# A two-layer graph kernel in fp32: row sums of layer 0 on ScalarE, block transposes moved into the projection, sums of v in the room of the blocks

## The chip, the cores and the metric

The kernel runs on one core of one Trainium2 chip. A core has five engines with queues of their own, each worked off in order: TensorE (PE, matrix products; its weight loads are shown as PEld), VectorE (DVE), ScalarE (ACT), GpSimd (POOL) and SyncE (SP, which here only issues DMA transfers). The metric is the device time of one execution in microseconds (us), the median of several runs. Before the change it is 1717.73 us (three runs, 1717.66 to 1717.78).

## The reference

Inputs are x (64 graphs x 256 nodes x 512 features), a 0/1 adjacency matrix adj (256 x 256), three 512 x 512 weights Wq, Wk, Wv for layer 0, and a weight and a bias for layer 1. All is fp32.

```python
# layer 0
h = relu(layernorm(x))
q, k, v = h @ Wq.T, h @ Wk.T, h @ Wv.T
rel = adj.T * (q @ k.T)                      # 256 x 256 for each graph
rel = rel / norm(rel, axis=2)                # by rows
x = x + rel @ v
# layer 1
h = relu(layernorm(x))
x = x + (adj @ h) @ weight + bias
```

## The kernel before

The 64 graphs are worked off as 32 pairs. A tile of a pair has 128 partitions and, for x and h, four chunks of 512 elements (two graphs x two halves of the nodes). Wq and Wk are folded into one matrix M beforehand (`before_pairs`), so a pair needs G = M h, v, the scores h G, attention, and for layer 1 a gather (adj h) and a mix (times the weight).

Most products run as Winograd's 2 x 2 scheme: seven block products instead of eight (`winograd_steps`). They accumulate in three PSUM banks in the order bank_a, bank_c, bank_a, bank_c, bank_a, bank_b, bank_a; after each product the bank is emptied at once by `take`, by a ScalarE copy if it is the first value of its output block, else by a VectorE add. A later product into the same bank waits until that read is done. The operands of the scheme are sums and differences of blocks, four VectorE steps each: `right_operands` (L133 to L136) and `left_factors` (L158 to L161).

After a start (`first_pairs`) a steady step (`steady(i)`, 28 of them) works on several pairs at once, in this order on TensorE:

- `attend_and_v(i)`: attention of pair i and v of pair i+1, product by product in turn (L465 and L217, tiles of v and of x_ring)
- `scores(i+1)` (L229)
- `project_g(i+2)` (L205)
- `gather(i)` (L522, tiles py, yt)
- `mix(i)` (L217, tiles yt, ys, w)

`last_pairs` ends the run. The order on TensorE, VectorE and ScalarE is the program's own, written by hand: each stage takes a table `side`, and the work listed under slot n is issued right behind the stage's product n and its `take`. So a list such as `2: [end] + sums[1:2]` is a piece of an engine's queue, and an instruction that waits holds up all that stands behind it on its engine.

What else runs in a steady step: the norm of layer 0 for pair i+3 (`ln0`: bn_stats and bn_aggr on VectorE, L248 and L249, root on ScalarE, L253, relu on ScalarE, L260), the norm of layer 1 for pair i (`ln1`, the same lines, then an upper and a lower half of h: a ScalarE cast, L499, and a VectorE difference, L503) and the bias add on GpSimd (L495). h of pair i+3 is transposed in two moves: `place_blocks` sends its 32 x 32 blocks to transposed places in the tile `blocks` by 16 DMA transfers on SP's queue (L299), and `transpose_blocks` turns each on VectorE (L309, eight steps), giving `ht`; its four sums are called `sums`. The scores are masked (L375), their rows squared and summed on ScalarE (L380, into a tile `square` that nothing reads), scaled (L389), placed by 16 transfers (L396) and turned (L399).

Tiles come from pools. Tiles with one tag share one room (pool `work`): "hy" holds h of a pair and then yt; "ys" holds the sums of g (`g_operands`) and those of yt; "gt" holds the sums of v (`attend_operands`, tile vt). The adjacency matrix has a room of its own.

Of the kernel before, what the change touches and what calls it, by code (L numbers as in the profile page):

```python
# [19 lines left out]
def kernel(  # L20
# [36 lines left out]
    nc = tc.nc  # L57
    P = 128
    B, N, D = x.shape
    DC = D // P  # L60
    NC = N // P
# [29 lines left out]
    wq_sb = work.tile([P, DC, D], F32, tag="g", name="wq_sb")  # L91
    wk_sb = twice.tile([P, DC, D], F32, tag="v", name="wk_sb")
    wv_sb = work.tile([P, DC, D], F32, tag="h2", name="wv_sb")
    adj_sb = const.tile([P, NC, N], F32, name="adj_sb")
    w_sb = const.tile([P, DC, D], F32, name="w_sb")
    bias_bc = const.tile([P, D], F32, name="bias_bc")
    nc.scalar.dma_start(out=adj_sb, in_=adj.rearrange("(c p) n -> p c n", p=P))
# [20 lines left out]
    def flat(t):  # L118
        return t.rearrange("p b c d -> p (b c) d")
# [24 lines left out]
    def run(steps):  # L144
        for step in steps:
            step()
# [90 lines left out]
    def norm(src):  # L237
# [25 lines left out]

        return [(lambda c=c: chunk(c)) for c in range(TC)], root, end, relu


    def ln0(i):
# [7 lines left out]
        return chunks, root, end, [(lambda c=c: relu(h[:, c, :], c)) for c in range(TC)]  # L275

    def new_ht(i):
        return twice.tile([P, DC, NC, NB * P], F32, tag="ht", name=f"ht_{i}")
# [49 lines left out]
        winograd(product_tokens_moving(HL[i], m_right), take, side)  # L328
        G[i] = g

    def g_operands(i, tag="ys"):

        g, t = G[i], work.tile([P, 3, HC, HT_], F32, tag=tag, name=f"gt_{i}")
        G[i], steps = right_operands(
            lambda j, k: g[:, j * HC : (j + 1) * HC, k], [t[:, n] for n in range(3)]
        )
        return steps

    def v_products(i):
# [15 lines left out]
    def scores(i, side={}, by_matmul=False):  # L355


        left, right = HL.pop(i), G.pop(i)
        rel = work.tile([P, NB, NC, N], F32, tag="rel", name=f"rel_{i}")
        placed = work.tile([P, NB, NC, NC, P], F32, tag="placed", name=f"placed_{i}")  # L360
        turned = work.tile([P, NB, NC, NC, P], F32, tag="turned", name=f"turned_{i}")
        square = work.tile([P, N], F32, tag="square", name=f"square_{i}")
        rn = small.tile([P, NB, NC], F32, tag="rn", name="rn")
        R[i] = turned, rel

        def take(t, k, bank, first):
            dst = rel[:, :, k, ts(t, P)]
            src = bank[:, :HT_].rearrange("p (b m) -> p b m", b=NB)
            if first:
                nc.scalar.copy(dst, src)  # L370
            else:
                nc.vector.tensor_add(dst, src, dst)  # L372

        def mask(k):
            nc.vector.tensor_mul(  # L375
                rel[:, :, k], rel[:, :, k], adjt_sb[:, k : k + 1, :].to_broadcast([P, NB, N])
            )

        def square_sum(b, k):
            nc.scalar.activation(square, rel[:, b, k], AF.Square, accum_out=rn[:, b, k : k + 1])  # L380

        def root():
            nc.scalar.activation(rn, rn, AF.Sqrt)

        def inverse():
            nc.vector.reciprocal(rn, rn)

        def scale(b, k):
            nc.scalar.activation(rel[:, b, k], rel[:, b, k], AF.Copy, scale=rn[:, b, k : k + 1])  # L389

        def place():
            rv = rel.rearrange("p b k (t m) -> p (b k t) m", m=P)
            pv = placed.rearrange("p b k t n -> p (b k t) n")
            for j in range(P // S):
                for k in range(P // S):
                    nc.sync.dma_start(out=pv[ts(j, S), :, ts(k, S)], in_=rv[ts(k, S), :, ts(j, S)])  # L396

        def turn(b, k):
            nc.vector.transpose(turned[:, b, :, k], placed[:, b, k])  # L399

        def each(f):
            return [(lambda b=b, k=k: f(b, k)) for k in range(NC) for b in range(NB)]

        def turn_at_once():
            for b in range(NB):
                pt = ps_m.tile([P, T], F32, tag="pm", name="pr")
                for t in range(NC):
                    for k in range(NC):
                        nc.tensor.transpose(
                            pt[:, ts(t * NC + k, P)], rel[:, b, k, ts(t, P)], ident  # L410
                        )
                nc.scalar.copy(turned[:, b].rearrange("p t k n -> p (t k n)"), pt)

        winograd(product_of_tokens(left, right), take, side)
        if by_matmul:
            masks = [lambda: mask(0), lambda: mask(1)]
# [26 lines left out]
    def attend_operands(i):  # L443


        turned, rel = R.pop(i)
        v, t = V.pop(i), work.tile([P, 3, NB, HD], F32, tag="gt", name=f"vt_{i}")
        room = rel.rearrange("p b k m -> p (b k m)")
        left, left_steps = left_factors(
            lambda n, m: turned[:, :, m, n],  # L450
            [room[:, ts(j, HT_)].rearrange("p (b n) -> p b n", b=NB) for j in range(3)],
        )
        right, right_steps = right_operands(
            lambda m, k: v[:, :, m, ts(k, HD)], [t[:, n] for n in range(3)]
        )
        R[i] = left, right
        return right_steps, left_steps
# [98 lines left out]
    def layer_1(parts):  # L556

        root, end, relus, uppers, lowers = parts
        return {
            0: [root, end, relus[0], relus[1]],  # L560
            1: [uppers[0], uppers[1], lowers[0]],
            2: [relus[2], lowers[1]],
            3: [relus[3], uppers[2], uppers[3]],
            4: [lowers[2]],
            5: [lowers[3]],
        }

    def before_pairs():
# [42 lines left out]
        def take(t, k, bank, first):  # L611
# [12 lines left out]
            1: [left_steps[2], right_steps[2]],  # L624
            2: stats[0:2] + [lambda: load(1, nc.scalar)],
            3: [left_steps[3]] + stats[2:4] + [root, right_steps[0], lambda: load(2, nc.scalar)],
            4: [transpose_wv, end] + relus + [right_steps[3]],
            5: m_steps[0:3],
            6: m_steps[3:4],
        }, early=True)  # L630

# [26 lines left out]
    def first_pairs(exact):  # L658
# [46 lines left out]
        if exact:  # L705
# [2 lines left out]
            1: [inverse], 3: scales + [place], 4: turned3[0:1], 5: turned3[1:2], 6: turned3[2:4],  # L708
        }))
        v_steps, rel_steps = attend_operands(1)  # L710
        y_steps = gather(0, exact, {
            0: turned3[4:8], 1: v_steps[0:1], 2: v_steps[1:3], 3: v_steps[3:4],
        })
        run(y_steps[0:2])
        mix(0, {0: y_steps[2:3], 1: y_steps[3:4], 4: turns, 5: rel_steps})
        return sums3

    def steady(i, exact, sums):

        gs = g_operands(i + 1)
        stats0, root0, end0, relus0 = ln0(i + 3)
        stats, root, end, relus, uppers, lowers = ln1(i, exact)
        halves = [stats[b * NC + t] for t in range(NC) for b in range(NB)]
        attend_and_v(i, {
            0: stats0[0:2], 1: stats0[2:4] + [root0], 2: [end0, relus0[0]] + gs[0:2],
            3: relus0[1:2] + gs[2:3], 4: relus0[2:3] + gs[3:4], 5: relus0[3:4] + sums[0:1],
            6: halves[0:2],
        })  # L730
        place_blocks(i + 3)
        masks, squares, norm_root, inverse, scales, place, turns = scores(i + 1, {
            0: halves[2:3], 1: halves[3:4] + [root], 2: [end] + sums[1:2], 3: relus[0:1],
            4: relus[1:2], 5: uppers[0:1], 6: uppers[1:2] + sums[2:4],
        })
        v_steps, rel_steps = attend_operands(i + 1)
        project_g(i + 2, {
            0: masks[0:1] + lowers[0:1] + relus[2:3],
            1: masks[1:2] + lowers[1:2] + relus[3:4],
            2: uppers[2:4] + squares[0:2] + v_steps[0:1],  # L740
            3: lowers[2:3] + squares[2:4] + [norm_root],
            4: lowers[3:4] + [inverse] + scales + [place],
            5: v_steps[1:2],
            6: v_steps[2:4],
        })
# [82 lines left out]
```

## Time and profile before

| | |
|---|---|
| median of 3 runs | 1717.73 us |
| profiled execution | 1717.2 us |
| its span, first to last instruction | 1715.1 us |
| granted TensorE clock | 0.999 |
| busy share: PE, PEld | 99%, 89% |
| busy share: DVE, ACT, POOL | 79%, 39%, 12% |
| one steady step (attend stage starts at 857.58 us, the next at 909.9) | 52.3 us |
| its stages: attend and v, scores, project_g, gather, mix | 18.1, 6.3, 12.1, 3.7, 12.1 us |

All times inside the execution count from the start of the span. In a row of the profile, "out<-in" are tiles by their names in the program, "L252" is a line of the kernel, and in lists of waits the engine and tile left of the arrow waited for those on its right. An engine's busy share says little by itself here: what matters is which engine another one waits for at a given point.

### The profile page before, as it was taken

What the parts mean: (1) busy time and instruction counts of PE and PEld (TensorE: products, weight loads), DVE (VectorE), ACT (ScalarE), POOL (GpSimd) and SP (SyncE); (2) the same over time, 40 slices, a digit from 0 to 9 for tenths busy, and PEclk for the clock granted to TensorE, in tenths of its full rate; (3) what the DMA queues carried; (4) which work ended last, traced back from release to release, by engine and by line L of the source; (5) the groups of instructions that cost most, each with busy time, mean ns of one, the idle gap of its engine ahead of it and who ended that gap; (6) DMA issues with size and microseconds to landing.
All of it is one profiled execution on the core that took longest, in us unless ns stands there. A gap on an engine that the chain in (4) does not pass through costs nothing.

```text
span 1715.1 us, 24952 instructions
## 1 busy us (share of the span) xinstructions
PE 1702.2 (99%) x9170; PEld 1518.2 (89%) x9170; DVE 1360.1 (79%) x2672; ACT 663.3 (39%) x1387; POOL 201.2 (12%) x167
## 2 busy tenths in 40 slices
PE   9999999999999999999999999999999999999998
PEld 7979998989898999889898989998889989899986
DVE  6778888878888888888787888888888888887655
ACT  4434433444333344334443333443343433334331
POOL 0011100111101111001111011110011110011111
PEclk9999999999999999999999999999999999999999
DMA  7423333233332233332233322333322334222011
GB/s 239 65 33 80 77 86 76 51 59 80 81 86 66 45 74 77 86 77 56 53 81 80 87 67 48 71 76 85 78 59 49 81 80 87 68 53 41 28 24 63
DMA packets 425972, 122.34 MB, mean 71 GB/s; under 512 B 398064, under 2 KB 399344, under 8 KB 425840
## 3 DMA queue, kind: packets, MB, share of 16 engines
q1 hardware_dynamic: 413248, 80.28, 25.1%
q0 software_dynamic: 8432, 32.51, 5.0%
q10 hardware_dynamic: 4160, 7.87, 1.3%
q8 instruction: 74, 1.21, 0.3%
q14 instruction: 58, 0.48, 0.1%
HBM read 38.27 MB, written 33.55 MB: 42 GB/s over the span
## 4 chain that ended last, share of the span: by engine, by line
PE 96%; DVE 3%; ACT 0%; DMA 0%; issue 0%; ACTq 0%; DVEq 0%
PE bank_a L217 25%; PE bank_c L217 13%; PE bank_a L205 13%; PE py L522 7%; PE bank_a L229 7%; PE bank_b L217 7%; PE bank_c L205 6%; PE bank_a L465 6%; PE bank_c L229 3%; PE bank_b L205 3%; PE bank_c L465 3%; PE bank_b L229 2%; PE bank_b L465 1%; DVE st L248 1%; PE pu L430 0%; DMA wk_sb<-in_L_gnn_Wk_dram 0%
## 5 line engine op out<-in xcount | busy, mean ns | idle before, releaser
L346 ACT COPY v<-bank_a 128x512 f32<-128x512 f32 x96 | 56.2, 586 | 676.6 <-PE bank_a L217 676.6
L495 POOL TENSOR_TENSOR x_ring<-x_ring,bias_bc 128x512 f32<-128x512 f32 x128 | 176.3, 1396 | 822.6 <-DVE rel L372 548.8
L248 DVE BATCH_NORM_STATS2 st<-x_ring 128x6 f32<-128x512 f32 x256 | 171.5, 670 | 0.4
L539 DVE TENSOR_TENSOR x_ring<-bank_a,x_ring 128x512 f32<-128x512 f32 x128 | 88.2, 689 | 57.9 <-PE bank_a L217 57.9
L522 PE MATMUL py<-adjt_r,h 128*128 128x256 f32 x1024 | 130.4, 285 | 0.0
L522 PEld LDWEIGHTS py<-adjt_r,h 128*128 128x128 f32 x1024 | 123.9, 189 | 1.6
L217 PE MATMUL bank_a<-w_t,ys 128*128 128x256 f32 x512 | 121.3, 380 | 1.7 <-DVE x_ring L539 1.7
L217 PE MATMUL bank_a<-wv_t,hs 128*128 128x256 f32 x512 | 121.0, 379 | 0.0
L205 PE MATMUL bank_a<-hs,m_t 128*128 128x256 f32 x512 | 121.0, 379 | 0.0
L260 ACT ACTIVATE h2c<-x_ring,nb,rs 128x512 f32<-128x512 f32 x128 | 100.6, 810 | 32.6 <-DVE h L503 25.9
L217 PEld LDWEIGHTS bank_a<-w_t,ys 128*128 128x128 f32 x512 | 95.7, 190 | 17.3 <-DVE x_ring L539 3.0
L217 PEld LDWEIGHTS bank_a<-wv_t,hs 128*128 128x128 f32 x512 | 97.4, 190 | 13.1
L205 PEld LDWEIGHTS bank_a<-hs,m_t 128*128 128x128 f32 x512 | 97.4, 190 | 13.1
L546 POOL DMA_DIRECT2D out_dram<-x_ring x31 | 24.0, 773 | 671.2 <-issue 489.2
L503 DVE TENSOR_TENSOR h<-h2c,h 128x512 fp32r<-128x512 f32 x128 | 91.1, 711 | 5.6 <-ACT h L499 5.6
L526 ACT COPY yt<-py 128x512 f32<-128x512 f32 x128 | 75.1, 587 | 47.2 <-PE py L522 47.2
L260 ACT ACTIVATE h<-x_ring,nb,rs 128x512 f32<-128x512 f32 x124 | 91.0, 806 | 1.5 <-DVE nb L257 1.5
L309 DVE STREAM_TRANSPOSE ht<-blocks 128x256 f32<-128x256 f32 x248 | 84.8, 407 | 1.4 <-DMA blocks<-h 1.4
L539 DVE TENSOR_TENSOR x_ring<-bank_c,x_ring 128x512 f32<-128x512 f32 x64 | 44.2, 691 | 46.1 <-PE bank_c L217 46.1
L472 DVE TENSOR_TENSOR x_ring<-bank_a,x_ring 128x512 f32<-128x512 f32 x116 | 79.4, 685 | 1.3 <-PE bank_a L465 1.3
L499 ACT CAST h<-h2c 128x512 fp32r<-128x512 f32 x128 | 75.3, 616 | 0.0
L324 ACT COPY g<-bank_a 128x512 f32<-128x512 f32 x96 | 56.2, 586 | 43.2 <-PE bank_a L205 41.1
(175 smaller groups left out, 3669.4 us busy)
## 6 DMA issues: line engine op xcount, KB each, us to landing
blocks<-h SPq DMA_DIRECT2D x496, 64.0 KB, 2.3
out_dram<-x_ring POOLq DMA_DIRECT2D x31, 1024.0 KB, 4.7
x_ring<-in_x_dram SPq DMA_DIRECT2D x28, 1024.0 KB, 5.3
placed<-rel SPq DMA_DIRECT2D x496, 32.0 KB, 2.0
x_ring<-in_x_dram ACTq DMA_DIRECT2D x4, 1024.0 KB, 5.3
wq_sb<-in_L_gnn_Wq_dram SPq DMA_DIRECT2D x4, 256.0 KB, 5.0
wk_sb<-in_L_gnn_Wk_dram ACTq DMA_DIRECT2D x4, 256.0 KB, 6.3
wv_sb<-in_L_gnn_Wv_dram ACTq DMA_DIRECT2D x1, 1024.0 KB, 5.4
```

The lines of the kernel that those rows point to most:

```text
L205: nc.tensor.matmul(bank[:, e * HT_ : (e + 1) * HT_], right[n][:, d, ts(e, P)], left[n][:, d, :], start=(start and e == 0 and d == 0), stop ...
L217: nc.tensor.matmul(bank[:, b * HD : (b + 1) * HD], left[n][:, d, ts(b, P)], right[n][:, d, :], start=(start and b == 0 and d == 0), stop=( ...
L229: nc.tensor.matmul(bank[:, ts(b, P)], right[n][:, d, ts(b, P)], left[n][:, d, ts(b, P)], start=(start and b == 0 and d == 0), stop=(d == H ...
L248: nc.vector.bn_stats(st[:, c, :], src[:, c, :])
L260: nc.scalar.activation(dst, src[:, c, :], AF.Relu, bias=nb[:, c : c + 1], scale=rs[:, c : c + 1])
L309: nc.vector.transpose(ht[:, d, half].rearrange("p (b n) -> p b n", b=NB), by_half[:, :, half, d])
L465: nc.tensor.matmul(bank[:, ts(b, HD)], left[n][:, b], right[n][:, b], start=(start and b == 0), stop=True, skip_group_check=True,)
L472: nc.vector.tensor_add(dst, bank.rearrange("p (b e) -> p b e", b=NB), dst)
L495: nc.gpsimd.tensor_tensor(xt[:, c, :], xt[:, c, :], bias_bc, ALU.add)
L503: nc.vector.tensor_sub(dst[:, 1, c, :], whole_h[c], dst[:, 0, c, :].bitcast(F32))
L522: nc.tensor.matmul(pm[:, d, :], left[:, b * NC + m, ts(d0 + d, P)], right, start=(n == 0), stop=(n == len(terms) - 1),)
L539: nc.vector.tensor_add(xt[block], bank.rearrange("p (b e) -> p b e", b=NB), xt[block])
```

## The change

The change has five parts, and no arithmetic of the result is dropped.

1. In the steady steps the norm of layer 0 (`ln0_by_scalar`) no longer uses bn_stats. ScalarE makes the row sums, by a Copy with an accumulator output, and the sums of squared differences, by Square with the negative mean as bias. VectorE makes the mean, the variance's floor, the reciprocal and the bias from [128 x 4] values. The passes write into h's own room.
2. In the steady steps the four sums of h of pair i+2 (`sums`) all stand in the attend stage's slots 4 to 6. Before, the first stood in slot 5 and the others in slots 2 and 6 of the scores.
3. The eight block transposes stand in slots 5 and 6 of `project_g` (before: in the gather), and the four sums of v stand in the gather (before: in slots 2, 5 and 6 of `project_g`).
4. The sums of v lie in the tile `blocks`, not in "gt". The squares of the scores are written into `placed`, not into `square`. The adjacency matrix shares the room "placed".
5. At the ends: Wv's transposes behind the sixth product of the setup's scheme instead of the fifth, with M's first sums; sums of v of the first pair in its mix instead of its gather; in `layer_1` the lower halves one or two slots later; two sums of yt of the last pair but one behind products of its mix instead of inside the last attention.

```diff
-    adj_sb = const.tile([P, NC, N], F32, name="adj_sb")
+    adj_sb = work.tile([P, NC, N], F32, tag="placed", name="adj_sb")
...
+    def norm_by_scalar(src, scratch):
...
+        def total(c):
+            nc.scalar.activation(scratch[:, c, :], src[:, c, :], AF.Copy, accum_out=sm[:, c : c + 1])
+        def mean():
+            nc.vector.tensor_single_scalar(sm, sm, -1.0 / D, op=ALU.mult)
+        def square(c):
+            nc.scalar.activation(
+                scratch[:, c, :], src[:, c, :], AF.Square, bias=sm[:, c : c + 1],
+                accum_out=sq[:, c : c + 1],
+            )
+        def root():
+            nc.vector.tensor_scalar(sq, sq, 0.0, EPS * D, op0=ALU.max, op1=ALU.add)
+            nc.scalar.activation(rs, sq, AF.Sqrt, scale=1.0 / D)
+        def end():
+            nc.vector.reciprocal(rs, rs)
+            nc.vector.tensor_tensor(nb, sm, rs, ALU.mult)
...
+    def spare_blocks():
+        room = blocks.rearrange("p c d e -> p (c d e)")
+        return [room[:, ts(n, 512)].rearrange("p (a b) -> p a b", a=2) for n in range(3)]
...
         def square_sum(b, k):
-            nc.scalar.activation(square, rel[:, b, k], AF.Square, accum_out=rn[:, b, k : k + 1])
+            nc.scalar.activation(
+                placed[:, b, k].rearrange("p t n -> p (t n)"), rel[:, b, k], AF.Square,
+                accum_out=rn[:, b, k : k + 1],
+            )
...
-        v, t = V.pop(i), work.tile([P, 3, NB, HD], F32, tag="gt", name=f"vt_{i}")
+        v, t = V.pop(i), spare_blocks()
...
     def layer_1(parts):
...
-            1: [uppers[0], uppers[1], lowers[0]],
-            2: [relus[2], lowers[1]],
-            3: [relus[3], uppers[2], uppers[3]],
+            1: [uppers[0], uppers[1]],
+            2: [lowers[0], relus[2], lowers[1], relus[3]],
+            3: [uppers[2], uppers[3]],
...
     def before_pairs():
...
-            4: [transpose_wv, end] + relus + [right_steps[3]],
-            5: m_steps[0:3],
+            4: [end] + relus + [right_steps[3]],
+            5: m_steps[0:3] + [transpose_wv],
...
     def first_pairs(exact):
...
-        y_steps = gather(0, exact, {
-            0: turned3[4:8], 1: v_steps[0:1], 2: v_steps[1:3], 3: v_steps[3:4],
-        })
+        y_steps = gather(0, exact, {0: turned3[4:6], 1: turned3[6:7], 2: turned3[7:8]})
         run(y_steps[0:2])
-        mix(0, {0: y_steps[2:3], 1: y_steps[3:4], 4: turns, 5: rel_steps})
+        mix(0, {
+            0: y_steps[2:3], 1: y_steps[3:4] + v_steps[0:1], 2: v_steps[1:2], 3: v_steps[2:4],
+            4: turns, 5: rel_steps,
+        })
...
     def steady(i, exact, sums):
...
-        stats0, root0, end0, relus0 = ln0(i + 3)
+        totals, mean, row_squares, root0, end0, relus0 = ln0_by_scalar(i + 3)
...
         attend_and_v(i, {
-            0: stats0[0:2], 1: stats0[2:4] + [root0], 2: [end0, relus0[0]] + gs[0:2],
-            3: relus0[1:2] + gs[2:3], 4: relus0[2:3] + gs[3:4], 5: relus0[3:4] + sums[0:1],
-            6: halves[0:2],
+            0: totals[0:2], 1: totals[2:4] + [mean], 2: row_squares[0:2] + gs[0:2],
+            3: row_squares[2:4] + [root0, end0] + gs[2:3], 4: relus0[0:2] + gs[3:4] + sums[0:1],
+            5: relus0[2:4] + sums[1:3], 6: sums[3:4] + halves[0:2],
         })
         place_blocks(i + 3)
         masks, squares, norm_root, inverse, scales, place, turns = scores(i + 1, {
-            0: halves[2:3], 1: halves[3:4] + [root], 2: [end] + sums[1:2], 3: relus[0:1],
-            4: relus[1:2], 5: uppers[0:1], 6: uppers[1:2] + sums[2:4],
+            0: halves[2:3], 1: halves[3:4] + [root], 2: [end], 3: relus[0:1],
+            4: relus[1:2], 5: uppers[0:1], 6: uppers[1:2],
         })
-        v_steps, rel_steps = attend_operands(i + 1)
+        turned, sums = transpose_blocks(i + 3)
         project_g(i + 2, {
...
-            2: uppers[2:4] + squares[0:2] + v_steps[0:1],
+            2: uppers[2:4] + squares[0:2],
...
-            5: v_steps[1:2],
-            6: v_steps[2:4],
+            5: turned[0:3],
+            6: turned[3:8],
         })
-        turned, sums = transpose_blocks(i + 3)
-        y_steps = gather(i, exact, {0: turned[0:3], 1: turned[3:6], 2: turned[6:8]})
+        v_steps, rel_steps = attend_operands(i + 1)
+        y_steps = gather(i, exact, {n: v_steps[n : n + 1] for n in range(4)})
...
     def last_pairs(exact, sums):
...
-        gs = g_operands(c, "gt")
+        gs = g_operands(c, spare_blocks())
...
-        attend(c, {n: [stats[n], y_steps[n]] for n in range(TC)}, rn)
-        mix(b, layer_1(parts))
+        attend(c, {0: [stats[0], y_steps[0]], 1: [stats[1], y_steps[1]], 2: [stats[2]], 3: [stats[3]]}, rn)
+        mix(b, by_slot({0: y_steps[2:3], 1: y_steps[3:4]}, layer_1(parts)))
```

More of the change, by code (lines that the diff above doesn't have):

```diff
@@ L264, in norm, with relu, each @@
         return [(lambda c=c: chunk(c)) for c in range(TC)], root, end, relu
+    def norm_by_scalar(src, scratch):
+        sm = small.tile([P, TC], F32, tag="sm", name="sm")
+        sq = small.tile([P, TC], F32, tag="sq", name="sq")
+        rs = small.tile([P, TC], F32, tag="rs", name="rs")
+        nb = small.tile([P, TC], F32, tag="nb", name="nb")
+        def total(c):
[13 more added lines that the diff above has]
+            nc.vector.tensor_tensor(nb, sm, rs, ALU.mult)
+        def relu(c):
+            nc.scalar.activation(
+                scratch[:, c, :], src[:, c, :], AF.Relu, bias=nb[:, c : c + 1], scale=rs[:, c : c + 1]
+            )
+        def each(f):
+            return [(lambda c=c: f(c)) for c in range(TC)]
+        return each(total), mean, each(square), root, end, each(relu)
     def ln0(i):
@@ L275, in ln0, with ln0_by_scalar @@
         return chunks, root, end, [(lambda c=c: relu(h[:, c, :], c)) for c in range(TC)]
+    def ln0_by_scalar(i):
+        H[i] = work.tile([P, TC, D], F32, tag="hy", name=f"h_{i}")
+        return norm_by_scalar(flat(X[i]), H[i])
     def new_ht(i):
@@ L329, in project_g, with g_operands @@
         G[i] = g
[L331 to L336, printed above, removed]
+    def spare_blocks():
+        room = blocks.rearrange("p c d e -> p (c d e)")
+        return [room[:, ts(n, 512)].rearrange("p (a b) -> p a b", a=2) for n in range(3)]
+    def g_operands(i, room=None):
+        g = G[i]
+        if room is None:
+            t = work.tile([P, 3, HC, HT_], F32, tag="ys", name=f"gt_{i}")
+            room = [t[:, n] for n in range(3)]
+        G[i], steps = right_operands(lambda j, k: g[:, j * HC : (j + 1) * HC, k], room)
         return steps
@@ L361, in scores @@
         turned = work.tile([P, NB, NC, NC, P], F32, tag="turned", name=f"turned_{i}")
-        square = work.tile([P, N], F32, tag="square", name=f"square_{i}")
         rn = small.tile([P, NB, NC], F32, tag="rn", name="rn")
@@ L379, in square_sum @@
         def square_sum(b, k):
-            nc.scalar.activation(square, rel[:, b, k], AF.Square, accum_out=rn[:, b, k : k + 1])
+            nc.scalar.activation(
+                placed[:, b, k].rearrange("p t n -> p (t n)"), rel[:, b, k], AF.Square,
+                accum_out=rn[:, b, k : k + 1],
+            )
         def root():
@@ L453, in attend_operands @@
         right, right_steps = right_operands(
-            lambda m, k: v[:, :, m, ts(k, HD)], [t[:, n] for n in range(3)]
+            lambda m, k: v[:, :, m, ts(k, HD)], t
         )
@@ L710, in first_pairs @@
         v_steps, rel_steps = attend_operands(1)
-        y_steps = gather(0, exact, {
-            0: turned3[4:8], 1: v_steps[0:1], 2: v_steps[1:3], 3: v_steps[3:4],
-        })
-        run(y_steps[0:2])
-        mix(0, {0: y_steps[2:3], 1: y_steps[3:4], 4: turns, 5: rel_steps})
+        y_steps = gather(0, exact, {0: turned3[4:6], 1: turned3[6:7], 2: turned3[7:8]})
+        run(y_steps[0:2])
+        mix(0, {
+            0: y_steps[2:3], 1: y_steps[3:4] + v_steps[0:1], 2: v_steps[1:2], 3: v_steps[2:4],
+            4: turns, 5: rel_steps,
+        })
         return sums3
```

## The prediction

> **What bounds the kernel now.** I read first the page's busy times, then the list of what TensorE waited for, then the timeline of one steady step. The page's first part:
>
> ```profile
> PE 1702.2 (99%) x9170; PEld 1518.2 (89%) x9170; DVE 1360.1 (79%) x2672; ACT 663.3 (39%) x1387; POOL 201.2 (12%) x167
> ```
>
> Only 13 us of the span are not TensorE work. Its waits in the whole run (line and tile waiting, releaser, us in total, times, longest):
>
> ```profile
> PE bank_a L217 <- DVE x_ring L539: 1.7, 3, 0.9
> PE bank_c L217 <- DVE yt L159: 1.4, 1, 1.4
> PE bank_a L217 <- DVE m_sb L617: 0.8, 1, 0.8
> ```
>
> By the timeline these three stand at the two ends: m_sb at 22.9 us, yt at 114.0 (first pair), x_ring at 1662.8, 1684.0 and 1688.1 (last pairs). The same list cut to 200 to 1640 us is empty: the 28 steady steps keep TensorE fed. So the change can win a few us at the ends, and in the steady step it can only lose. How much room is there? The timeline of the step whose attend stage starts at 857.58 us (start, duration, engine, line, operation; in brackets the idle time before it and who ended it):
>
> ```profile
> 875.13 0.68 DVE L248 BATCH_NORM_STATS2 st<-x_ring 128x6 f32<-128x512 f32 x1
> ...
> 878.44 0.17 DVE L252 TENSOR_SCALAR rs<-mv 128x4 f32<-128x4 f32 x1
> 878.65 0.20 ACT L253 ACTIVATE rs<-rs 128x4 f32<-128x4 f32 x1 [0.58 <-DVE rs L252]
> 878.76 0.35 ACT L370 COPY rel<-bank_a 128x256 f32<-128x256 f32 x1
> 879.28 1.06 PE L229 MATMUL bank_a<-hs,gt 128*128 128x128 f32 x8
> ...
> 881.61 1.64 DVE L160 TENSOR_TENSOR hs<-ht 128x512 f32<-128x512 f32 x1
> ...
> 898.58 0.69 DVE L159 TENSOR_TENSOR yt<-yt 128x512 f32<-128x512 f32 x1
> 899.42 1.97 PE L217 MATMUL bank_c<-w_sb,yt 128*128 128x256 f32 x8
> ```
>
> Two near misses. **Scores:** ScalarE's queue has the root of layer 1's norm (L253) in front of the copy that empties bank_a after the third product (L370). The fifth product accumulates into that bank and waits for the copy. The copy ends at 879.11, the product starts at 879.28: 0.17 us of slack, and the copy follows VectorE's L252 (878.44 to 879.11, 0.67 us later). **Mix:** the second product waits for VectorE's L159, which ends at 899.27; TensorE comes at 899.42, 0.15 us later.
>
> **What the Trainium skill says.** "ScalarE: Activation LUTs", section "Rules for kernel authors", budgets about 0.3 us per ACTIVATE and 0.83 ns an element, an estimate of 0.73 us for 512; here four relus take 2.93 us and one 0.81, so 0.71 from start to start: it agrees. Its section "Table sets" has one load per switch of set; the page shows one ACT_TABLE_LOAD in all, with Square, Relu and Sqrt already in use, so I charge none. "GPSIMD Engine Reference", section "Specifications", says that GpSimd's SBUF interfaces are shared with VectorE and contend with VectorE instructions that have two SBUF inputs. The trace agrees: L160 above took 1.64 us, usually 0.68, while GpSimd's bias adds ran (880.20 to 882.70).
>
> **Part 1: row sums of layer 0.** Each steady step drops four bn_stats pairs from VectorE (0.80 each, start to start) and gives ScalarE four totals and four squares of 512 elements with an accumulator. The trace has that form with 256 only:
>
> ```profile
> 888.87 0.42 ACT L380 ACTIVATE square<-rel 128x256 f32<-128x256 f32 x1
> 889.18 0.19 ACT L380 ACTIVATION_READ_ACCUMULATOR square<-rel 128x1 f32 x1
> 889.40 0.42 ACT L380 ACTIVATE square<-rel 128x256 f32<-128x256 f32 x1
> ```
>
> 0.53 from start to start, against 0.40 for a 256-element ACTIVATE without accumulator (L389, four in 1.71). So 512 elements cost 0.71 + 0.13 = 0.84, an estimate; ends kept: 0.70 (accumulator free) and 1.00. ScalarE has room in sum (39% busy, 8 x 0.84 = 6.7 us more in a step of 52.3, less nothing). What counts is that VectorE's queue now holds three instructions that wait for ScalarE: the mean, the variance and the reciprocal.
>
> The walk, on TensorE's times above. v's copies of bank_a and bank_c end ScalarE's slots at 860.85 and 863.44, so totals start 860.85, 861.69, 863.44, 864.28 and the last is read out at 865.1. VectorE, idle from 861.9, takes the mean, then the bank_a add, two sums of g, the bank_c add (865.2 to 867.7), and v's bank_c add, ready at 868.21. Squares start behind v's copy of bank_a (865.55): 866.03, 866.87, 867.71, 868.55, read out at 869.35. Then variance 869.39, root on ScalarE 869.60, reciprocal 869.83, bias 870.05: VectorE resumes at 870.13. The adds held behind the two waits are still in time: TensorE comes back to attend's bank_a at 867.94 and 873.12, and they end by 865.9 and 871.4.
>
> **Part 2: sums of h moved forward.** The built program's order has, after that bias and before layer 1's L252: third sum of g, attend bank_a, v bank_a, fourth sum of g, sum 1 of h, attend bank_b, v bank_b, sums 2 and 3, attend bank_a, sum 4, then four bn_stats pairs. Before, only sum 1 stood there; 2 to 4 came after L252 (879.18, 881.61, 883.28). Eleven instructions: ten at 0.60 and one dependent at 0.72 make 6.72, so the pairs start at 876.85 (875.13 before) and L252 at 876.85 + 3.31 = 880.16, 1.72 us later. Less the slack of 0.17: TensorE stops **1.55 us** at the fifth product of scores. Everything behind moves with it, relus, masks and squares too, so nothing is won back. Bounds: even with ScalarE free, v's adds fix 868.21, 870.73 and 873.32, and the pairs start at 876.44: 1.15. With 1.00 per square: 2.2.
>
> **Part 3: transposes into G, sums of v into the gather.** Before, VectorE made one v sum at 886.29, three from 893.13, then eight transposes in 2.72 us. Now after g's bank_b add (892.52) come eight transposes from 893.13 (0.326 apart, the last ends at 895.81), four dependent v sums (0.72 apart: 895.84, 896.56, 897.28, 898.00), then L158 at 898.60 and L159 at 899.32, ending at 900.01 against TensorE's 899.42: **0.6 us** at the second mix product. Bounds 0.4 and 0.8 (a step earlier the same sum gives 0.5; GpSimd is idle there). The next sums (y3, y4) then keep ahead.
>
> **Part 4: the room of the blocks.** The t operands of v lie in blocks, so SP's first block transfer waits for the last attend product that reads them, ending at 874.15, instead of for h (868.99). h is done by 870.2 + 2.9 = 873.1, no later. Sixteen issues take 10.95 us and a landing 2.3: 887.4. The transposes come at 893.13 + 1.55 and the gather's first copy, which reuses h's room, later still: 7 us of cover, cost nothing. Behind them on SP stand the placed transfers, issued near 893.9 as before; GpSimd's queue keeps its order. Squares written into placed: its last reader is one stage back, nothing. adj_sb sharing that tag is read only in the first 7 us, nothing.
>
> **Part 5: the ends.** Moving wv's 16 transposes (1.74 us) behind the sixth setup product uncovers L133 (to 18.89): product 6 starts 18.93 and the last at 22.40 instead of 22.85: -0.4. In the first pair L159 loses three v sums in front of it: -1.5. In layer_1 the lower halves no longer stand before the bank_a add: -0.55 and -0.6 (waits at 1662.8 and 1688.1). In attend(c) two y sums move behind the first mix add: about -0.4 of the 1.07 lost at 1684. Together -3.4, bounds -4.5 and -1.5.
>
> **Sum.** 28 steps x (1.55 + 0.6) = 60.2; minus 3.4 = +56.8. The profiled execution took 1717.2 (span 1715.1 and 2.1 around it): 1774. The median shown is 0.5 above it: 1774.5, said as 1774.
>
> **Rivals.** *A, the stall in scores alone:* ScalarE's accumulating passes cost near 0.70 and the mix hides L159; the ACTIVATE rows leave room for it, L159's 0.15 slack speaks against it. 28 x 1.2 - 3.4 = +30: 1748. *B, ScalarE dearer and SBUF contention:* passes near 1.0, and v or y sums meeting GpSimd's adds as L133 did (1.76 instead of 0.68). 28 x (2.2 + 0.8) - 2 = +82: 1800. *C, the other side:* taking 3.6 us of norm work from VectorE outweighs the three sums and L252 comes by 878.61 (878.44 plus the slack). Then only the ends count: 1714. For that VectorE would have to resume by 868.6 instead of 870.13, but v's bank_c add, ahead of it in the queue, ends at 868.9 and three hops over ScalarE follow. *D, no effect:* scores and mix fit the slacks by 0.1 us and setup gives nothing: 1717.
>
> **Chances.** Forecast 0.70 (its own range 1760 to 1790), A 0.14, B 0.10, C 0.04, D 0.02. The range 1748 to 1794 takes the forecast's bounds, 28 x 1.6 - 4.5 and beyond to A, and most of B, and leaves out about 0.15. Faster by over 0.2% (about what a measurement of this kernel can tell from none) 0.04, within it 0.02, slower 0.94.
>
> **What would show it.** After: a group "PE bank_a <- ACT rel" or "<- DVE" in TensorE's waits, 28 times, about 1.5 us each, and "PE bank_c <- DVE yt" 28 times about 0.6; steps of about 54.4 us instead of 52.3; ACTIVATE with accumulator of 512 elements 0.84 apart; blocks transfers starting just after the attend stage's last product, and no wait of the transposes for them; no waits at 114.0 and in the last two mixes. The prediction is wrong if the variance on VectorE comes by 868.9, if TensorE's fifth scores product has another releaser, or if the mix shows no wait.

## The result and the profile after

The changed kernel takes 1774.59 us (median of 4 runs, 1774.08 to 1775.5) against 1717.70 us before (median of 4 runs): a ratio of 1.0332, 95% interval 1.0315 to 1.035. It is slower by 56.9 us. The forecast was 1774, +56.8. The profiled execution took 1774.38 us, with a span of 1772.1 us.

Busy times on the page of the changed kernel:

```profile
PE 1713.6 (97%) x9170; PEld 1519.9 (86%) x9170; DVE 1225.9 (69%) x2476; ACT 804.5 (45%) x1835; POOL 187.7 (11%) x167
```

VectorE is busy 134 us less, ScalarE 141 us more, and the kernel is slower: these two shares do not tell which way the time went. Then the shares of the chain of work that ended last, by engine (before, TensorE had 96% of it and VectorE 3%):

```profile
PE 62%; DVE 29%; ACT 7%; issue 2%; DVEq 0%; DMA 0%
```

The chain now leaves TensorE in every step. The list of TensorE's waits (line and tile waiting, releaser, us in total, times, longest) says where:

```profile
PE bank_a L229 <- ACT rel L417: 29.4, 28, 1.1
PE bank_c L217 <- DVE yt L159: 18.9, 28, 0.8
...
PE bank_a L217 <- DVE wk_t L133: 0.4, 1, 0.4
```

Both predicted groups are there, 28 times each. The three waits for x_ring in the last pairs, the one for m_sb and the single one of the first pair are no longer listed; one for wk_t in the setup is new. The list counts idle time by modelled ends; what the time feels is the distance between the starts of two products. That is read from the timeline of one steady step, whose attend stage starts at 885.20 us (start, duration, engine, line, operation; in brackets the idle time and its releaser). VectorE first, from the variance of layer 0's norm to layer 1's L252:

```profile
896.61 0.17 DVE L287 TENSOR_SCALAR sq<-sq 128x4 f32<-128x4 f32 x1
897.05 0.18 DVE L291 RECIPROCAL rs<-rs 128x4 f32<-128x4 f32 x1 [0.27 <-ACT rs L288]
897.27 0.16 DVE L292 TENSOR_TENSOR nb<-sm,rs 128x4 f32<-128x4 f32 x1
897.35 0.68 DVE L135 TENSOR_TENSOR gt<-g 128x512 f32<-128x512 f32 x1
...
900.95 0.68 DVE L396 TENSOR_TENSOR v<-bank_b,v 128x512 f32<-128x512 f32 x1
...
904.07 0.68 DVE L248 BATCH_NORM_STATS2 st<-x_ring 128x6 f32<-128x512 f32 x1
...
907.39 0.17 DVE L252 TENSOR_SCALAR rs<-mv 128x4 f32<-128x4 f32 x1
```

From 897.35 to 904.07 VectorE has no gap: the eleven instructions of the forecast, in 6.72 us. Now ScalarE and TensorE behind them in the same step, and VectorE and TensorE in its mix:

```profile
907.60 0.20 ACT L253 ACTIVATE rs<-rs 128x4 f32<-128x4 f32 x1 [1.91 <-DVE rs L252]
907.71 0.35 ACT L417 COPY rel<-bank_a 128x256 f32<-128x256 f32 x1
...
906.01 1.06 PE L229 MATMUL bank_c<-hs,g 128*128 128x128 f32 x8
908.11 1.16 PE L229 MATMUL bank_a<-hs,gt 128*128 128x128 f32 x8 [1.05 <-ACT rel L417]
...
928.40 0.69 DVE L159 TENSOR_TENSOR yt<-yt 128x512 f32<-128x512 f32 x1
926.76 1.89 PE L217 MATMUL bank_a<-w_sb,yt 128*128 128x256 f32 x8
929.24 1.97 PE L217 MATMUL bank_c<-w_sb,yt 128*128 128x256 f32 x8 [0.59 <-DVE yt L159]
```

The copy of bank_a starts the moment the norm root is out of its way, and the fifth scores product starts 0.05 us after the copy's end. Two scores products are normally 0.89 us apart and here 2.10: 1.21 us lost. The sixth product then starts 1.00 behind the fifth (909.11), another 0.11 lost. Two mix products are normally 1.73 apart and here 2.48: 0.75 in this step, 0.84 on average over the 28. For the mix, these are the lines before, where the first product started at 897.69 and L159 0.89 us behind it (here 1.64):

```profile
897.69 1.89 PE L217 MATMUL bank_a<-w_sb,yt 128*128 128x256 f32 x8
898.58 0.69 DVE L159 TENSOR_TENSOR yt<-yt 128x512 f32<-128x512 f32 x1
899.39 1.59 PEld L217 LDWEIGHTS bank_c<-w_sb,yt 128*128 128x128 f32 x8 [0.21 <-issue]
899.42 1.97 PE L217 MATMUL bank_c<-w_sb,yt 128*128 128x256 f32 x8
```

The steady step is 54.5 us long (52.3 before). From the first product of a stage to the first of the next, as a mean of the 28 steps, the scores take 7.56 instead of 6.25 and the mix 13.00 instead of 12.14; the gather (3.88, before 3.92; the 3.7 of the table ahead is one step, cut at another instruction) and the other two stages are as they were.

### The profile page after: what moved, and what is told of

The parts are those of the page before. It is cut to its first block, busy times and chain, and to the rows that moved or that the text cites. A ratio compares the mean times of both kernels' runs of the same rounds, so it can differ in the third digit from the quotient of the medians.

```text
span 1772.1 us, 25292 instructions
## 1 busy us (share of the span) xinstructions
PE 1713.6 (97%) x9170; PEld 1519.9 (86%) x9170; DVE 1225.9 (69%) x2476; ACT 804.5 (45%) x1835; POOL 187.7 (11%) x167
## 3 DMA queue, kind: packets, MB, share of 16 engines
q8 instruction: 74, 1.21, 0.3%
## 4 chain that ended last, share of the span: by engine, by line
PE 62%; DVE 29%; ACT 7%; issue 2%; DVEq 0%; DMA 0%
PE bank_a L217 17%; PE bank_c L217 10%; PE bank_a L205 10%; PE bank_c L205 6%; ACT h L281 4%; DVE ht L351 4%; DVE st L248 4%; PE bank_a L229 4%; PE bank_b L217 4%; PE bank_b L205 3%; PE bank_a L515 3%; DVE x_ring L522 3%; DVE v L396 2%; PE bank_b L229 2%; PE bank_c L515 1%
## 5 line engine op out<-in xcount | busy, mean ns | idle before, releaser
L545 POOL TENSOR_TENSOR x_ring<-x_ring,bias_bc 128x512 f32<-128x512 f32 x128 | 162.8, 1283 | 846.6 <-ACT h2c L260 846.6
L589 DVE TENSOR_TENSOR x_ring<-bank_a,x_ring 128x512 f32<-128x512 f32 x128 | 87.9, 687 | 44.0 <-PE bank_a L217 44.0
L368 DVE TENSOR_TENSOR g<-bank_c,g 128x512 f32<-128x512 f32 x32 | 22.1, 691 | 120.8 <-PE bank_c L205 120.8
L229 PE MATMUL bank_a<-hs,gt 128*128 128x128 f32 x496 | 68.4, 281 | 29.4 <-ACT rel L417 29.4
L248 DVE BATCH_NORM_STATS2 st<-x_ring 128x6 f32<-128x512 f32 x144 | 96.4, 669 | 0.4
L229 PEld LDWEIGHTS bank_a<-hs,gt 128*128 128x128 f32 x496 | 60.2, 191 | 34.7 <-ACT rel L417 34.7
L295 ACT ACTIVATE h<-x_ring,nb,rs 128x512 f32<-128x512 f32 x112 | 82.0, 802 | 12.4 <-DVE nb L292 12.4
```

The source lines that it names most:

```text
L229: nc.tensor.matmul(bank[:, ts(b, P)], right[n][:, d, ts(b, P)], left[n][:, d, ts(b, P)], start=(start and b == 0 and d == 0), stop=(d == H ...
L248: nc.vector.bn_stats(st[:, c, :], src[:, c, :])
L295: nc.scalar.activation(scratch[:, c, :], src[:, c, :], AF.Relu, bias=nb[:, c : c + 1], scale=rs[:, c : c + 1])
L545: nc.gpsimd.tensor_tensor(xt[:, c, :], xt[:, c, :], bias_bc, ALU.add)
L589: nc.vector.tensor_add(xt[block], bank.rearrange("p (b e) -> p b e", b=NB), xt[block])
```

## The experiments

The theory: three sums moved ahead of layer 1's norm make the copy of bank_a late (scores), four sums of v moved ahead of L159 make the mix late, the two are independent, and the other parts cost nothing. The rivals: ScalarE's new passes cause the scores stall; or GpSimd and VectorE collide; or one stall would reappear elsewhere when the other is taken away. Each ratio below is taken against runs of the kernel before made along with it (1717.3 to 1717.7 us).

**Undoing one stall at a time, in the changed kernel.** First, the sums of h go back to where they stood:

```diff
-            3: row_squares[2:4] + [root0, end0] + gs[2:3], 4: relus0[0:2] + gs[3:4] + sums[0:1],
-            5: relus0[2:4] + sums[1:3], 6: sums[3:4] + halves[0:2],
+            3: row_squares[2:4] + [root0, end0] + gs[2:3], 4: relus0[0:2] + gs[3:4],
+            5: relus0[2:4] + sums[0:1], 6: halves[0:2],
...
-            0: halves[2:3], 1: halves[3:4] + [root], 2: [end], 3: relus[0:1],
-            4: relus[1:2], 5: uppers[0:1], 6: uppers[1:2],
+            0: halves[2:3], 1: halves[3:4] + [root], 2: [end] + sums[1:2], 3: relus[0:1],
+            4: relus[1:2], 5: uppers[0:1], 6: uppers[1:2] + sums[2:4],
```

> The changed kernel with only the sums of h moved back: in the steady step sum 1 stands in the attend stage's slot 5, sum 2 in the scores' slot 2 behind the end of the norm, sums 3 and 4 in slot 6. ScalarE still makes the row sums. My theory (three sums ahead of VectorE's L252 make the scores wait): L252 falls back to about 20.5 us after the start of the attend stage, no wait of TensorE in the scores, the mix still waits 0.87: 1774.6 - 28 x 1.32 = 1737.6 us. Rival (the three hops over ScalarE are what makes VectorE late): the wait stays, 1770 to 1775 us.

Measured 1738.07 us, ratio 1.0118 (1.0102 to 1.0133). TensorE's longest waits in it:

```profile
PE bank_c L217 <- DVE yt L159: 18.8, 28, 0.7
PE pf L639 <- DVE low_max L637: 1.4, 1, 1.4
```

The scores stall is gone, with ScalarE's norm still in place, and the mix stall is as it was. Second, the sums of v go from the gather into the mix:

```diff
-        y_steps = gather(i, exact, {n: v_steps[n : n + 1] for n in range(4)})
+        y_steps = gather(i, exact)
...
-        mix(i, {0: y_steps[2:3], 1: y_steps[3:4], 4: turns, 5: rel_steps})
+        mix(i, {
+            0: y_steps[2:3], 1: y_steps[3:4] + v_steps[0:1], 2: v_steps[1:2], 3: v_steps[2:4],
+            4: turns, 5: rel_steps,
+        })
```

> The changed kernel with only the four sums of v moved from the gather to slots 1 to 3 of the mix, behind the first two sums of yt. My theory (four dependent sums of 0.72 in front of L159 make the second mix product wait): no wait at the mix, the scores still wait: 1774.6 - 28 x 0.87 = 1750.2 us. Rival (VectorE has too much work between projection and the next attend stage, so the sums are late wherever they stand): the wait moves to the end of the mix or the second attend product, 1765 to 1775 us.

Measured 1749.14 us, ratio 1.0182 (1.0167 to 1.0198). In TensorE's waits the mix is gone and the scores stand alone:

```profile
PE bank_a L229 <- ACT rel L417: 29.5, 28, 1.1
```

Third, both edits together, as in the two diffs above:

> Both edits at once: sums of h back in the scores, sums of v in the mix. My theory: no steady wait is left, a steady step takes 52.3 us as before and the gains at the two ends show: 1774.6 - 28 x 2.19 = 1713.3 us. Rival (room of the blocks, later block transfers or ScalarE's load cost something of their own): 1718 us or more.

Measured 1713.45 us, ratio 0.9975 (0.9967 to 0.9983), with no wait left in the steady steps; the top of the list is the setup:

```profile
PE pz L624 <- POOL warm L105: 1.0, 1, 1.0
PE pf L639 <- DVE low_max L637: 1.0, 1, 1.0
```

So neither stall hides another. Fourth, only the order in front of the copy changes: the norm root of layer 1 moves from the scores' slot 1 to slot 2, behind the copy.

```diff
-            0: halves[2:3], 1: halves[3:4] + [root], 2: [end], 3: relus[0:1],
+            0: halves[2:3], 1: halves[3:4], 2: [root, end], 3: relus[0:1],
```

> The changed kernel with only the root step of layer 1's norm (L252 on VectorE, L253 on ScalarE) moved from the scores' slot 1 to slot 2, so behind ScalarE's copy that empties bank_a. VectorE is as late as before. My theory (the product waits because the copy stands behind a root that waits for VectorE): the fifth product no longer waits, and what is left is the last product's wait for VectorE's add of the fifth, 0.1 to 0.4 us a step: 1774.6 - 28 x 1.0 = 1746 us, 1742 to 1752. Rival (VectorE's lateness itself holds TensorE, through its adds from bank_c and bank_a): the wait moves but keeps its size, 1768 to 1775 us.

Measured 1746.91 us, ratio 1.0171 (1.0155 to 1.0186). The wait for the copy is gone from the list, which now begins with the mix:

```profile
PE bank_c L217 <- DVE yt L159: 16.8, 28, 0.7
```

The sums of h are as early here as in the changed kernel, and L252 as late. What stalls TensorE is therefore the copy standing behind the root in ScalarE's queue, not VectorE's lateness by itself. The lateness still costs something by another way. In this run's timeline the last scores product waits for VectorE's add of bank_a, which stands behind L252 to L257 in VectorE's queue:

```profile
895.58 0.41 DVE L419 TENSOR_TENSOR rel<-bank_a,rel 128x256 f32<-128x256 f32 x1
...
894.90 1.06 PE L229 MATMUL bank_b<-ht,g 128*128 128x128 f32 x8
896.04 1.16 PE L229 MATMUL bank_a<-ht,gt 128*128 128x128 f32 x8
```

These two products are 1.14 apart instead of 0.89: 28 x 0.25 = 7 of the 8.8 us that this run has more than the one with the sums back. The product behind them starts another 0.11 late, about 3 us in all, so this account is about 1 us over what was measured.

**One part alone, on the kernel before.** Part 1, the norm on ScalarE (`ln0_by_scalar` as in the change):

```diff
-        stats0, root0, end0, relus0 = ln0(i + 3)
+        totals, mean, row_squares, root0, end0, relus0 = ln0_by_scalar(i + 3)
...
-            0: stats0[0:2], 1: stats0[2:4] + [root0], 2: [end0, relus0[0]] + gs[0:2],
-            3: relus0[1:2] + gs[2:3], 4: relus0[2:3] + gs[3:4], 5: relus0[3:4] + sums[0:1],
+            0: totals[0:2], 1: totals[2:4] + [mean], 2: row_squares[0:2] + gs[0:2],
+            3: row_squares[2:4] + [root0, end0] + gs[2:3], 4: relus0[0:2] + gs[3:4],
+            5: relus0[2:4] + sums[0:1],
```

> The kernel before with only part 1: row sums of layer 0 by ScalarE in the steady steps, sums of h and all else where they stood. My theory (the norm's move costs TensorE nothing, and gains nothing either, since VectorE was early enough): no steady wait, 1717.7 us, 1716 to 1720. Rival (three hops over ScalarE make VectorE late): waits in the scores, 1730 us or more.

Measured 1717.26 us against 1717.34, ratio 0.9998 (0.999 to 1.0007): nothing. Part 2, the sums of h in the attend stage:

```diff
-            3: relus0[1:2] + gs[2:3], 4: relus0[2:3] + gs[3:4], 5: relus0[3:4] + sums[0:1],
-            6: halves[0:2],
+            3: relus0[1:2] + gs[2:3], 4: relus0[2:3] + gs[3:4] + sums[0:1],
+            5: relus0[3:4] + sums[1:3], 6: sums[3:4] + halves[0:2],
...
-            0: halves[2:3], 1: halves[3:4] + [root], 2: [end] + sums[1:2], 3: relus[0:1],
-            4: relus[1:2], 5: uppers[0:1], 6: uppers[1:2] + sums[2:4],
+            0: halves[2:3], 1: halves[3:4] + [root], 2: [end], 3: relus[0:1],
+            4: relus[1:2], 5: uppers[0:1], 6: uppers[1:2],
```

> The kernel before with only part 2: all four sums of h in the attend stage's slots 4 to 6, the norm of layer 0 still by bn_stats on VectorE. My theory: L252 comes 1.3 us later (19.9+1.3 after the attend stage's start is 22.2), the fifth scores product waits 1.3 us: 1717.7 + 28 x 1.3 = 1754 us, 1748 to 1765. Rival (the sums hurt only together with ScalarE's row sums): 1717 to 1722.

Measured 1752.82 us, ratio 1.0206 (1.019 to 1.0221). (Before, L252 stands 20.86 us after the start of the attend stage, not 19.9; the 22.2 is right.) Here the norm of layer 0 is still bn_stats on VectorE, and TensorE's wait for the copy has the size that it has in the changed kernel:

```profile
PE bank_a L229 <- ACT rel L370: 29.4, 28, 1.1
```

Its timeline (the step whose scores start at 893.34 us) shows VectorE and what it waits for:

```profile
888.36 0.69 DVE L348 TENSOR_TENSOR v<-bank_a,v 128x512 f32<-128x512 f32 x1 [0.63 <-PE bank_a L217]
...
890.95 0.69 DVE L348 TENSOR_TENSOR v<-bank_b,v 128x512 f32<-128x512 f32 x1
...
897.40 0.17 DVE L252 TENSOR_SCALAR rs<-mv 128x4 f32<-128x4 f32 x1
...
889.02 1.89 PE L217 MATMUL bank_b<-wvt_sb,ht 128*128 128x256 f32 x8
```

TensorE's bank_b product of v ends at 890.91 and its add starts at 890.95; what stands behind that add on VectorE cannot come earlier. L252 comes 4.06 us after the start of the scores here (median of the steps), 4.06 in the changed kernel, and 2.73 before. Part 3 and the first edit of part 4: the transposes in G, the sums of v in the gather and in the blocks' room (`spare_blocks` as in the change):

```diff
-        v, t = V.pop(i), work.tile([P, 3, NB, HD], F32, tag="gt", name=f"vt_{i}")
+        v, t = V.pop(i), spare_blocks()
...
-            5: v_steps[1:2],
-            6: v_steps[2:4],
+            5: turned[0:3],
+            6: turned[3:8],
...
-        y_steps = gather(i, exact, {0: turned[0:3], 1: turned[3:6], 2: turned[6:8]})
+        y_steps = gather(i, exact, {n: v_steps[n : n + 1] for n in range(4)})
```

> The kernel before with only parts 3 and 4 for v: block transposes in project_g's slots 5 and 6, sums of v in the gather and in the room of the blocks. My theory: the second mix product waits 0.87 us a step: 1717.7 + 28 x 0.87 = 1742 us, 1738 to 1748; the block transfers start at the end of the attend stage without anybody waiting for them. Rival (the later block transfers are what is waited for): the transposes show waits for DMA.

Measured 1741.29 us, ratio 1.0139 (1.0123 to 1.0155), with the mix stall alone (19.8 us in 29 waits, one of them the old one of the first pair). The transposes wait for transfers 0.2 us in the whole run, so the later transfers are not what is waited for. Part 5, the ends (of its four edits, shown with the change, the one of the first pair):

```diff
-            0: turned3[4:8], 1: v_steps[0:1], 2: v_steps[1:3], 3: v_steps[3:4],
-        })
+        y_steps = gather(0, exact, {0: turned3[4:6], 1: turned3[6:7], 2: turned3[7:8]})
...
-        mix(0, {0: y_steps[2:3], 1: y_steps[3:4], 4: turns, 5: rel_steps})
+        mix(0, {
+            0: y_steps[2:3], 1: y_steps[3:4] + v_steps[0:1], 2: v_steps[1:2], 3: v_steps[2:4],
```

> The kernel before with only part 5, the reordering at the two ends. My theory: the waits at 22.9, 114, 1662.8, 1684 and 1688 us shrink from 4.7 to about 1.1 us in sum: 1714.2 us, 1713 to 1715.5. Rival (the freed time is lost again at the next wait of the start or the tail): 1717 to 1718.

Measured 1713.83 us, ratio 0.9979 (0.997 to 0.9988). These four runs give -0.1, +35.5, +24.0 and -3.5, together +55.8, of the +56.9 of the whole change. The other two edits of part 4 (the squares in `placed`, the adjacency matrix in that room) were not run alone; the changed kernel with both stalls undone has them and is level with the ends alone (1713.45 and 1713.83 us).

**The price of an accumulating pass.** The forecast took 0.84 us for 512 elements; the changed kernel shows less. Rows of ScalarE's timeline in it, for the norm's squares and for the scores' squares:

```profile
894.37 0.71 ACT L281 ACTIVATE h<-x_ring,sm 128x512 f32<-128x512 f32 x1
894.99 0.19 ACT L281 ACTIVATION_READ_ACCUMULATOR h<-x_ring,sm 128x1 f32 x1
895.08 0.71 ACT L281 ACTIVATE h<-x_ring,sm 128x512 f32<-128x512 f32 x1
...
918.21 0.40 ACT L427 ACTIVATE placed<-rel 128x256 f32<-128x256 f32 x1
918.51 0.19 ACT L427 ACTIVATION_READ_ACCUMULATOR placed<-rel 128x1 f32 x1
918.61 0.41 ACT L427 ACTIVATE placed<-rel 128x256 f32<-128x256 f32 x1
```

0.71 and 0.40 from start to start: the price without an accumulator. Before, the 256-element passes stood 0.53 apart, but all of them wrote the one tile `square`. To see whether that is the reason, the changed kernel's passes of the norm get one common scratch tile instead of slices of h:

```diff
+        lost = work.tile([P, D], F32, tag="lost", name="lost")
...
-            nc.scalar.activation(scratch[:, c, :], src[:, c, :], AF.Copy, accum_out=sm[:, c : c + 1])
+            nc.scalar.activation(lost, src[:, c, :], AF.Copy, accum_out=sm[:, c : c + 1])
...
-                scratch[:, c, :], src[:, c, :], AF.Square, bias=sm[:, c : c + 1],
+                lost, src[:, c, :], AF.Square, bias=sm[:, c : c + 1],
```

> The changed kernel, with ScalarE's totals and squares of the norm all writing one scratch tile instead of four slices of h, so that each pass writes over the one ahead of it. In the changed kernel the squares came 0.70 us apart and the scores' squares, which write separate places, 0.40; in the kernel before the scores' squares wrote one tile and came 0.53 apart. Theory: the 0.13 between 0.40 and 0.53 was each pass's wait on the one that it writes over, so here the passes of the norm come about 0.83 apart, VectorE resumes about 0.4 to 0.5 later, the norm root is as much later, and the stall at the fifth scores product grows by about 0.45 in each of 28 steps: 1774.6 + 13 = about 1787. Rival: the 0.13 belonged to something else (the form of 256 elements, or the code around it), the passes stay at 0.70: 1774.6.

Measured 1786.22 us, ratio 1.04 (1.0382 to 1.0417): 11.6 us more than the changed kernel, where the theory said 13 and the rival 0. ScalarE's timeline in it:

```profile
900.49 0.72 ACT L282 ACTIVATE lost<-x_ring,sm 128x512 f32<-128x512 f32 x1
901.12 0.19 ACT L282 ACTIVATION_READ_ACCUMULATOR lost<-x_ring,sm 128x1 f32 x1
901.34 0.72 ACT L282 ACTIVATE lost<-x_ring,sm 128x512 f32<-128x512 f32 x1
```

The squares are 0.85 apart, the totals 0.82 (0.62 in the changed kernel). The reading of the accumulator begins just as in the changed kernel; it is the next pass that starts later. Here it starts 0.03 us behind the end of the reading (901.12 + 0.19 to 901.34), as the 256-element passes before did (889.18 + 0.19 to 889.40); in the changed kernel it starts 0.09 ahead of that end (894.99 + 0.19 against 895.08). The packed trace agrees: each pass onto the common tile waits for a semaphore that ScalarE itself counts up at the end of each reading. So the addition is a wait for the pass that is written over, and not the price of the accumulator. And TensorE's wait grows:

```profile
PE bank_a L229 <- ACT rel L418: 41.4, 28, 1.5
```

L252 comes 4.49 us after the start of the scores instead of 4.06.

## Why the prediction was right, and where its terms were off

**The mechanism and the place of both stalls: right.** The copy behind the norm root in the scores, and L159 behind the sums of v in the mix, each 28 times, each with the releaser named; undoing one takes away that one alone, and undoing both leaves the gain at the ends. The sizes of both were off.

**Scores, 1.55 us a step: too much; the runs give about 1.3.** The part alone costs 35.5 us, 1.27 a step, and undoing it wins 1.30; the scores stage is 1.31 longer: 1.21 in front of the fifth product and 0.11 in front of the sixth. That 0.11 the forecast did not have. In a running stream the weights of a scores product start to load 0.11 us ahead of it (before, 879.17 and 879.28), but behind the stall together with it (both at 908.11). The term that was too large is the price of 0.84 for a pass with accumulator. The 0.13 that the forecast added to the 0.71 was read off rows of L380 where each pass wrote over the one ahead; with outputs in separate places it isn't there. "ScalarE: Activation LUTs", section "Rules for kernel authors", with its 0.3 us and 0.83 ns an element, gives an estimate of 0.73 for 512 elements; the 0.71 measured for a square agrees, with no addition for the accumulator. So VectorE resumed at 12.15 us after the start of the attend stage instead of the forecast's 12.55 (870.13 less 857.58), L252 was 1.33 us later than before instead of 1.72, and with 0.12 us of slack the stall is 1.21. Where the passes do cost 0.82 to 0.85, in the run with one scratch tile, L252 is 1.76 late, against the 1.72 of the forecast: the rest of the walk was sound.

The forecast had the other value as its lower bound, "even with ScalarE free, v's adds fix" the pairs, 1.15, and that is the one which holds: with bn_stats left on VectorE and the sums moved, L252 stands at the same 4.06 us. At 0.70 a pass, ScalarE's round trips and v's bank_b add release VectorE at practically the same moment. Part 1 as such therefore costs nothing here, alone or with part 2, and it earns nothing either, since TensorE never waited for what it takes away.

**Mix, 0.6 us a step: too little; the runs give 0.86.** Two terms were too favourable. The first is the slack. Before, L159 ended at 899.27 and the second product started at 899.42, and the forecast took the 0.15 between as room. After, TensorE waits for L159, which ends at 929.09, and starts at 929.24, again 0.15, and it is 0.15 in all 28 steps: this is what the product needs behind L159. The packed trace shows what differs from the scores, where it is 0.05: the mix product waits for two semaphores, one that VectorE counts up (L159) and one that TensorE itself counts up, and a semaphore instruction of its own stands on TensorE's queue in front of it (at 929.13, 0.05 us long), then the weights at 929.21. "Perfetto Trace Analysis", section "Identifying Dependency Chains", says that an instruction which waits for several engines may have such semaphore instructions placed ahead of it; the trace agrees. That this instruction makes the difference of 0.10 is read from the timeline; no run takes it away. The trace before has it too (at 899.31, the weights at 899.39), so in the step that the forecast was read from there was no room at all. In 18 of the 28 steps before, the product started 0.22 behind L159: room of 0.07.

The second is the delay. L159 was to start 0.74 us later. Counted from the first mix product it starts 0.75 later in the step shown, but 0.88 on average; the forecast took one step for all. The average of 0.88, less the 0.05 of room on average, is the 0.83 or 0.84 between the two products. The fifth scores product has no semaphore instruction ahead of it and starts 0.05 us behind the copy's end; this 0.05 is what comes off the 0.17 there.

**The errors cancel.** 1.27 + 0.86 = 2.13 us a step against the 2.15 of the forecast; 28 x 2.13 - 3.5 = +56.1. That the time was met within 1 us is luck: one term was some 0.25 too large, the other 0.26 too small. Rival A (scores alone, 1748) had the cheap passes right, and fell because the mix does not hide L159: the run with the mix repaired took 1749. Rival B needed passes near 1.0 and VectorE slowed by GpSimd. Neither came: "GPSIMD Engine Reference", section "Specifications", on the contention of the two agrees with the trace before, where 29 of the 65 instructions of L160 on 512 elements and 27 of L133 took 1.6 to 1.8 us instead of 0.68; after, one of L160 does and none of L133, since the moved sums no longer meet the bias adds (with the sums of h moved back, L160 is at 1.6 29 times again). The sums thus became cheaper, not dearer. Rival C asked for L252 by 878.61, and the floor set by v's adds kept it from that. Rival D is out by both stalls.

**Part 4, nothing: right as far as the runs show.** The transfers into blocks start at 901.84, just after the last attend product that reads them (900.74 + 1.03), and the transposes wait for a transfer once in the whole run, 1.8 us, without TensorE waiting for them. The trace after has one ACT_TABLE_LOAD, as assumed.

**Part 5, -3.4: right.** Alone it measures -3.5. (In `layer_1` only the first lower half moves to a later slot, by one; the last relu moves one slot ahead.) Summed from TensorE's timeline: the gap of 1.52 in the first pair is gone, as are those of 0.55 and 0.61 in the last mixes; the one of 1.07 in attend(c) has become 0.58 in two pieces; and in the setup a gap of 0.95 has given way to one of 0.61 (wk_t, L133, in the list above). That is -3.5.

## What to carry to other kernels

Before work is moved on an engine that nobody waits for, follow what stands behind it on the other engines' queues: three sums on VectorE made a norm root late, the root held up a copy on ScalarE, and the copy stopped TensorE. A gap in front of an instruction is room only by what is over its wait's own delay, and the spacing of a row is a price only if its instructions don't write over each other. Of several edits made as one, run each alone: here the ends gain 0.2%, two edits lose 2.1% and 1.4%, one does nothing, and the kernel before with the ends alone (1713.83 us) is level with the whole change without its two stalls (1713.45 us), the fastest that was run.

## What the runs showed of the hardware

- An ACTIVATE of 512 fp32 elements with an accumulator takes 0.62 (Copy) and 0.71 us (Square) from start to start when the outputs lie apart, and 0.82 and 0.85 when each writes over the one ahead and waits for it; for Square of 256 elements 0.40 and 0.53.
- From the end of the releasing instruction to the start of the waiting TensorE product: 0.05 us (a ScalarE copy, 908.06 to 908.11; a VectorE add in the run with the root moved, 895.99 to 896.04), but 0.15 us where a semaphore instruction stands ahead of the product (929.09 to 929.24).
- The eight matmuls of the scores product behind the stall took 1.16 us on the timeline, 1.06 in a running stream, and the next product started 1.00 behind it instead of 0.89.
- A VectorE instruction with two inputs of 128x512 took 1.6 to 1.8 us instead of 0.68 where GpSimd's bias adds ran beside it.
